# A perceiver layer on one core: weight conversions and lower halves moved from GpSimd to VectorE

## The chip, the core and the metric

The kernel runs on one core of a Trainium2 chip. A core has five engines, each with its own in-order queue of instructions: TensorE (PE in the profile; its weight loads are PEld), VectorE (DVE), ScalarE (ACT), GpSimd (POOL) and SyncE (SP, which here only issues DMA transfers). An instruction starts when those ahead of it on its engine are done and when the semaphores that it waits for, set by other engines or by transfers, have their values.

The metric is the device time of one execution in microseconds (us), lower is better. A run has several executions; the median is given.

## The reference

One perceiver layer: 4 sequences x of 256 tokens and width 256, and a context of 4096 tokens for each. Three blocks, each added to x: cross-attention of x on the context with 16 heads; causal linear attention with positive features; and a gated feed-forward whose weights are stored as int32. The features are the exponential of a clipped projection; the causal attention is the sum over earlier tokens of (qf . kf) v over the same sum without v; `_dequant` multiplies the integers by 1/127. Cut to what matters here:

```python
def _L0_attn_ref(x, Wqkv, bqkv, Wout, bout, omega, quad_nodes, quad_weights):
    ...
    qf = _features(q, omega, quad_nodes, quad_weights)
    kf = _features(k, omega, quad_nodes, quad_weights)
    ...
    return out @ Wout + bout

def _L0_ffn_ref(x, w_gate, w_up, w_down):
    wg = _dequant(w_gate, x.dtype)
    wu = _dequant(w_up, x.dtype)
    wd = _dequant(w_down, x.dtype)
    gate = jnp.einsum('bsd,hd->bsh', x, wg)
    up = jnp.einsum('bsd,hd->bsh', x, wu)
    h = jax.nn.silu(gate) * up
    return jnp.einsum('bsh,dh->bsd', h, wd)

x = x + _L0_xattn_ref(_layernorm(x, axis=-1), ctx_1024, ctx_1024, ...)
x = x + _L0_attn_ref(_layernorm(x, axis=-1), ...)
x = x + _L0_ffn_ref(_layernorm(x, axis=-1), ...)
```

## The kernel before, in words

**Cross-attention.** The 16 head groups (4 sequences x 4 groups of 4 heads; "units") are worked one after the other, each in 16 steps of 256 context tokens. A step n makes the scores `pt` of four heads (L1015 puts the shift in, L1024 the products), ScalarE their exponentials `e` (L1032), and TensorE the weighted values `pav` of the step before (L1046), which VectorE adds to the running sum `av` (L1060). In all units but the last TensorE also makes the maxima for a later unit (`pm`, L955, reduced by VectorE at L961). From about 887 us on, when the maxima are done, the steps of the last unit run, and the work of the later blocks is put between them. These steps are counted here from the first step of the last unit, which is step 0; the ones just before are -1, -2 and so on.

Two dictionaries place this work by step. `plan` holds pieces issued before the step's `pav`, `behind` pieces issued after the step's addition L1060. The order written in the program is the order on TensorE, ScalarE, VectorE and SyncE (it is written out by hand for these four); GpSimd's order follows from it.

**The weights.** The three int32 matrices of the feed-forward (gate, up, down) come in nine pieces of 128x512. `weight_load` (L435-437) has SyncE load piece n into one of two buffers, `wk_sb` for even n and `wv_sb` for odd n. `weight` (L439-441) converts it with GpSimd into `wfr`, in the matmul's type fp32r (integers up to 127 are exact in it). `weight_largest` (L447) has VectorE take the maximum of the converted piece; at the end the maximum of all is read back, and another feed-forward runs if a weight is too large. Piece n is converted in step `made[n]` = -2, -1, 1, 2, 4, 5, 7, 8, 10; right behind it the load of piece n+2 into the same buffer is issued; the maximum follows two steps later. Loads 0 and 1 are issued in step -4.

**Causal attention and feed-forward.** Behind the last unit runs a loop over n = 4 to 16 ("late steps") over the causal attention's head groups, with pieces of the feed-forward and of the output projection filled in (`first` and `fills`). `features` makes four banks `pf` (L314); VectorE clips them (L320), ScalarE takes the exponential (L321), and GpSimd scales the key half (L322). `attend` gives three pieces: the score matmuls `pa` (L340, L345), masked by ScalarE and GpSimd (copy L351, select L352) for two of the four and by VectorE (L357) for the others; the weighted values `po` (L366), copied to `avT` (L372); and, every second group, their transposes `pt_o` (L382) and the division into `att` (L387-389). `output` is two pieces: the transposes `tr_o` of `att` (L406), copied by ScalarE to `oT` (L407), and the projection `py` (L414), added to x by VectorE (L415).

`feed_forward(b)` for sequence b has `norm`, `turn` (transposes `tr_z`, split into an upper half by ScalarE, L621, and a lower half by VectorE, L622), `hidden(m)` for three pieces m and `down(i)` for two row tiles i. To keep fp32 accuracy with fp32r matmuls an activation is split in a half `hi` (rounded to fp32r) and a half `lo` (the rest), and both are multiplied. `hidden(m)`: TensorE makes `pg` and `pu` (L631), ScalarE the tanh (L636), VectorE two products (L637, L638) giving `th`; then GpSimd casts it to `hi` (L646) and subtracts for `lo` (L647), but for the very last piece, where ScalarE casts (L643) and VectorE subtracts (L644). `down(i)` does, for each side, the matmuls of six column blocks (L658), so twelve: first all six with `hi`, then all six with `lo`; blocks 2m and 2m+1 come from piece m. VectorE makes the output row tile (L665), and SyncE sends it (L666).

All matmul results lie in eight PSUM banks that are taken in turn: a new result waits until the one eight before it has been read.

Of the kernel before, what the change touches and what calls it, by code (L numbers as in the profile page):

```python
# [13 lines left out]
F32 = mybir.dt.float32  # L14
F32R = mybir.dt.float32r
I32 = mybir.dt.int32
AF = mybir.ActivationFunctionType
ALU = mybir.AluOpType
# [5 lines left out]
B, T, D = 4, 256, 256  # L24
# [12 lines left out]
NH = HID // P  # L37
# [4 lines left out]
def perceiver_layer(  # L42
# [5 lines left out]
    nc = tc.nc  # L48
# [159 lines left out]
    def bank(shape, name):  # L208

        return psum.tile(shape, F32, tag="b", name=name, bufs=8)  # L210
# [61 lines left out]
    def normed_pieces(tiles):  # L272

        some = nrm[:, tiles[0] : tiles[-1] + 1, :].rearrange("p t h -> p (t h)")
        made = []

        def clipped():
            nc.vector.tensor_scalar(some, some, 1e-24, None, ALU.max)
            y, (first, *others) = inverse_root(some)
            made.extend([*others, lambda: nc.vector.tensor_copy(some, y)])  # L280
            first()

        return [clipped] + 4 * [lambda: made.pop(0)()]
# [145 lines left out]
    def weight_piece(n):  # L429
        if not ws:  # L430
            wfr.append(keep.tile([P, 3 * KC * HID], F32R, tag="wff", name="wfr"))
            ws.extend(parted(wfr[0]))
        return wfr[0][:, n * CH : (n + 1) * CH]
# [4 lines left out]

    def weight(n):  # L439
        to, raw = weight_piece(n), place["raw"][n % 2]  # L440
        nc.gpsimd.tensor_scalar(to, raw.bitcast(I32), 1.0, 1.0, ALU.mult, ALU.mult)


    largest = keep.tile([P, 9], F32, tag="largest", name="largest")
# [34 lines left out]
    behind = {}  # L479

    def start_causal():
# [3 lines left out]
        n = 2 * (B - 1)  # L485
# [39 lines left out]
        def call(f, *args):  # L525
            return lambda: f(*args)
# [37 lines left out]
            15: [step4[1], norm0[3]],  # L564
        }

        made = (-2, -1, 1, 2, 4, 5, 7, 8, 10)
        for n, at in enumerate(made):
            behind.setdefault(at, []).append(call(weight, n))
            if n + 2 < len(made):  # L570
                behind.setdefault(at, []).append(call(weight_load, n + 2))
            behind.setdefault(at + 2, []).append(call(weight_largest, n))
        for b, at in enumerate((-18, -11, -3)):
            for i, piece in enumerate(normed_pieces((2 * b, 2 * b + 1))):
                plan.setdefault(at + i, []).insert(0, piece)
# [22 lines left out]
    def norm_late(z, tiles):  # L598
        for piece in layernorm(z, tiles, True):
            piece()  # L600
        nc.scalar.activation(spare, eps, AF.Tanh)
# [3 lines left out]
    def feed_forward(b):  # L605

        tiles = (2 * b, 2 * b + 1)
        z = work.tile([P, 2, D], F32, tag="z", name="z") if b > 0 else z0
        zT = work.tile([P, 2, KC, T], F32R, tag="zT", name="zT")
        halves_of = []  # L610

        def norm():
            norm_late(lambda t: z[:, t % 2, :], tiles)

        def turn():
            ps = bank([P, KC, 2, P], "tr_z")
            for j in range(2):
                for k in range(KC):
                    nc.tensor.transpose(ps[:, k, j, :], z[:, j, k * P : (k + 1) * P], ident)
            hi, lo = [zT[:, i].rearrange("p k (j t) -> p k j t", t=P) for i in range(2)]  # L620
            nc.scalar.copy(hi, ps)  # L621
            nc.vector.tensor_tensor(lo, ps, hi.bitcast(F32), ALU.subtract)  # L622

        def hidden(m):
            pg, pu = bank([P, 2, T], "pg"), bank([P, 2, T], "pu")
            for side in range(2):
                for ps, w in ((pg, ws[0]), (pu, ws[1])):
                    for i in range(2):
                        ns = slice((2 * m + i) * P, (2 * m + i + 1) * P)
                        for k in range(KC):  # L630
                            nc.tensor.matmul(  # L631
                                ps[:, i, :], lhsT=w[:, k, ns], rhs=zT[:, side, k, :],
                                start=i + k + side == 0, stop=i + k + side == KC + 1,
                            )
            th = work.tile([P, 2, T], F32, tag="th", name="th", bufs=3)
            nc.scalar.activation(th, pg, AF.Tanh, scale=0.5 / 127.0)  # L636
            nc.vector.scalar_tensor_tensor(th, th, 1.0, pg, ALU.add, ALU.mult)  # L637
            nc.vector.tensor_tensor(th, pu, th, ALU.mult)  # L638
            if m == 0:
                halves_of.append(work.tile([P, 2, NH, T], F32R, tag="hT", name="hT", bufs=1))  # L640
            hi, lo = [halves_of[0][:, i, 2 * m : 2 * m + 2, :] for i in range(2)]
            if b == B - 1 and m == NH // 2 - 1:
                nc.scalar.copy(hi, th)  # L643
                nc.vector.tensor_tensor(lo, th, hi.bitcast(F32), ALU.subtract)  # L644
            else:
                nc.gpsimd.tensor_copy(hi, th)  # L646
                nc.gpsimd.tensor_tensor(lo, th, hi.bitcast(F32), ALU.subtract)  # L647

        pds = {}

        def down(i, parts=range(NH)):
            t = tiles[i]
            if i not in pds:
                pds[i] = bank([P, D], "pd")
            pd = pds[i]
            for side in range(2):
                for n in parts:
                    nc.tensor.matmul(  # L658
                        pd, lhsT=halves_of[0][:, side, n, i * P : (i + 1) * P], rhs=ws[2][:, n, :],
                        start=n == 0 and side == 0, stop=n == NH - 1 and side == 1,  # L660
                    )
            if NH - 1 not in parts:
                return
            o = work.tile([P, D], F32, tag="o", name="o")
            nc.vector.scalar_tensor_tensor(o, pd, 0.5 / 127.0**3, xr[:, t, :], ALU.mult, ALU.add)  # L665
            nc.sync.dma_start(out=out[t * P : (t + 1) * P, :], in_=o)  # L666

        return norm, turn, hidden, down


    def feed_forward_any():
# [38 lines left out]
    with tc.manual_schedule(engines={ET.PE, ET.Activation, ET.DVE, ET.SP}):  # L710
        *divide15, project15 = finish
        NB = B * NQ
        norm3, turn3, qk3, sq3, v3, _ = causal_in(3, norm_late)
        ff = {0: feed_forward(0)}
        outputs = [output(b) for b in range(B)]
        ends = normed_pieces((6, 7))
        send, read, compare = weights_large()

        def call(f, *args):
            return lambda: f(*args)  # L720

        def norm(b):
            def begin():
                ff[b] = feed_forward(b)
                ff[b][0]()

            return begin

        def turn(b):
            return lambda: ff[b][1]()  # L730

        def hidden(b, m):
            return lambda: ff[b][2](m)

        def down(b, *args):
            return lambda: ff[b][3](*args)


        first = {
            6: divide15,  # L740
            8: [turn3],
            10: ends[2:] + [call(qk_normed, 6), call(qk_normed, 7)],
            13: [norm(2)],
        }
        fills = {
            4: [turn(0), call(features, 6)],
            5: [hidden(0, 0)],
            6: [call(features, 8), hidden(0, 1), project15, load_root],
            7: [norm3, hidden(0, 2)],
            8: [call(features, 10), call(qk3, 0), down(0, 0), outputs[1][0], call(qk3, 1), outputs[1][1], load_root],  # L750
            9: [norm(1), v3, call(sq3, 0), call(sq3, 1), down(0, 1), *ends[:2], turn(1)],
            10: [hidden(1, 0), call(qk_turned, 6), call(qk_turned, 7), send],
            11: [call(features, 12), hidden(1, 1), read],
            12: [hidden(1, 2), *outputs[2], load_root],
            13: [call(features, 14), down(1, 0), down(1, 1), turn(2)],
            14: [hidden(2, 0), compare],
            15: [hidden(2, 1)],
            16: [
                hidden(2, 2), *outputs[3], load_root, norm(3), down(2, 0), down(2, 1, range(3)), turn(3),
                down(2, 1, range(3, NH)), *[hidden(3, m) for m in range(NH // 2)], down(3, 0), down(3, 1),  # L760
            ],
        }
        steps = [attend(n) for n in range(NB)]
        for n in range(NQ, NB + 1):
            if n > NQ + 1:
                steps[n - 1][1]()
            if NQ < n < NB:
                steps[n][0]()
            for piece in first.get(n, []):
                piece()  # L770
            if n > NQ and n % 2 == 0:
                steps[n - 1][2]()
            for piece in fills[n]:
                piece()
# [676 lines left out]
```

## Time and profile before

| | |
|---|---|
| median of 3 runs | 1066.25 us (1063.87 to 1066.44) |
| the profiled execution's own time | 1064.58 us |
| its span, first to last instruction | 1062.9 us |
| mean granted TensorE clock | 0.992 of full |
| busy, of the span: PE, DVE, ACT, POOL | 97%, 86%, 76%, 20% |
| steps of the last unit with the weights | about 884 to 956 us |
| late steps and the last feed-forward | about 956 to 1058.9 us |
| `weight` L441 on POOL | 9 x 617 ns, 884.4 to 918.1 us |
| cast L646 and subtraction L647 on POOL | 11 x 612 ns and 11 x 1279 ns, 965.0 to 1054.0 us |

The profile is one execution, taken by the hardware's profiler. A timeline row gives start, duration, engine, line, operation, result and operands, their size, the count, and in brackets how long the engine had been idle before it and what ended that. Times count from the span's start. Matmuls overlap, so the ends of TensorE's rows are modelled; the distances of starts are what counts. The granted clock is the share of TensorE's full clock that the chip allowed in a stretch.

### The profile page before, as it was taken

What the parts mean: (1) busy time and instruction counts of PE and PEld (TensorE: products, weight loads), DVE (VectorE), ACT (ScalarE), POOL (GpSimd) and SP (SyncE); (2) the same over time, 40 slices, a digit from 0 to 9 for tenths busy, and PEclk for the clock granted to TensorE, in tenths of its full rate; (3) what the DMA queues carried; (4) which work ended last, traced back from release to release, by engine and by line L of the source; (5) the groups of instructions that cost most, each with busy time, mean ns of one, the idle gap of its engine ahead of it and who ended that gap; (6) DMA issues with size and microseconds to landing.
All of it is one profiled execution on the core that took longest, in us unless ns stands there. A gap on an engine that the chain in (4) does not pass through costs nothing.

```text
span 1062.9 us, 45087 instructions
## 1 busy us (share of the span) xinstructions
PE 1028.1 (97%) x19032; PEld 716.1 (67%) x19032; DVE 917.1 (86%) x1771; ACT 808.7 (76%) x1678; POOL 215.8 (20%) x308
## 2 busy tenths in 40 slices
PE   6999999999999999999999999999999998998997
PEld 3457667766776677667766776677666666566676
DVE  3998999999899999999999999999998996577775
ACT  3348888888888888888888888878885677785463
POOL 3422220032003200320032003201232102205343
PEclk8999999999999999999999999999999999999999
DMA  8666574366435753574357536643473301200000
GB/s 250 178 161 173 111 191 127 98 134 169 122 103 116 180 129 102 108 192 127 101 114 190 125 97 134 173 110 100 109 174 91 71 14 34 61 3 12 11 12 22
DMA packets 93791, 120.31 MB, mean 113 GB/s; under 512 B 49561, under 2 KB 58642, under 8 KB 93586
## 3 DMA queue, kind: packets, MB, share of 16 engines
q1 hardware_dynamic: 92738, 116.59, 44.0%
q8 instruction: 152, 2.49, 1.0%
q10 hardware_dynamic: 720, 0.79, 0.2%
q14 instruction: 53, 0.43, 0.2%
q0 software_dynamic: 128, 0.00, 0.0%
HBM read 76.25 MB, written 3.33 MB: 75 GB/s over the span
## 4 chain that ended last, share of the span: by engine, by line
PE 84%; DVE 9%; DMA 2%; ACT 1%; issue 1%; SPq 1%; POOL 1%; ACTq 0%; DVEq 0%; POOLq 0%
PE pc L184 23%; PE pav L1046 20%; PE pm L955 17%; PE pt L1024 11%; DVE mx L961 5%; PE pt L1015 4%; PE pqk L184 1%; PE pa L340 1%; PE po L366 1%; PE py L414 1%; PE pg L631 1%; PE pu L631 1%; PE py L184 1%; ACT feat L321 1%; PE pa L345 0%
## 5 line engine op out<-in xcount | busy, mean ns | idle before, releaser
L961 DVE TENSOR_REDUCE mx<-pm 128x1 f32<-128x512 f32 x787 | 506.1, 684 | 47.6 <-PE pm L955 44.1
L1032 ACT ACTIVATE e<-pt 128x512 f32<-128x512 f32 x1024 | 530.7, 614 | 15.7 <-PE pt L1024 15.2
L955 PE MATMUL pm<-kt,qa 32*128 32x512 f32 x2048 | 355.8, 426 | 9.2 <-DMA kt<-khl 5.7
L1024 PE MATMUL pt<-qa,kt 32*128 32x256 f32 x4096 | 283.3, 278 | 0.0
L1024 PEld LDWEIGHTS pt<-qa,kt 32*128 32x128 f32 x4096 | 270.4, 184 | 7.2
L1046 PE MATMUL pav<-e,v 128*32 128x256 f32 x4096 | 270.8, 381 | 0.7 <-issue 0.7
L955 PEld LDWEIGHTS pm<-kt,qa 32*128 32x128 f32 x2048 | 163.0, 191 | 120.6 <-ACT e L1032 82.3
L1015 PE MATMUL pt<-sh,ones 2*128 2x512 f32 x1024 | 226.0, 449 | 0.8 <-ACT e L1032 0.4
L1046 PEld LDWEIGHTS pav<-e,v 128*32 128x32 f32 x4096 | 129.2, 110 | 73.3 <-issue 4.7
L857 POOL CAST khl<-ku 128x512 fp32r<-128x512 f32 x63 | 38.5, 611 | 516.3 <-ACT ku L877 483.1
L184 PE MATMUL pc<-wff,wk_sb 128*32 128x256 f32 x2048 | 138.2, 392 | 0.0
L184 PE MATMUL pc<-wv_sb,wff 128*32 128x128 f32 x4096 | 137.6, 276 | 0.1
L965 ACT COPY copy<-pm 128x512 f32<-128x512 f32 x119 | 69.8, 587 | 65.8 <-PE pm L955 65.8
L965 ACT COPY wff<-pm 128x512 f32<-128x512 f32 x118 | 69.3, 587 | 65.9 <-PE pm L955 65.9
L184 PEld LDWEIGHTS pc<-wv_sb,wff 128*32 128x32 f32 x4096 | 104.4, 109 | 20.9 <-ACT copy L965 8.5
L1060 DVE TENSOR_TENSOR av<-pav,av 128x256 f32<-128x256 f32 x240 | 101.3, 422 | 15.9 <-PE pav L1046 6.4
L1015 PEld LDWEIGHTS pt<-sh,ones 2*128 2x128 f32 x1024 | 93.3, 182 | 13.1 <-ACT e L1032 3.5
L184 PEld LDWEIGHTS pc<-wff,wk_sb 128*32 128x32 f32 x2048 | 55.4, 111 | 46.6 <-ACT copy L965 8.7
L858 POOL TENSOR_TENSOR khl<-ku,khl 128x512 fp32r<-128x512 f32 x63 | 80.7, 1281 | 5.0
L961 DVE TENSOR_REDUCE mx<-copy 128x1 f32<-128x512 f32 x119 | 80.4, 675 | 0.0
L961 DVE TENSOR_REDUCE mx<-wff 128x1 f32<-128x512 f32 x118 | 79.6, 675 | 0.0
L877 ACT ACTIVATE ku<-pc,bk_sb 128x256 f32<-128x256 f32 x128 | 64.8, 508 | 14.9 <-PE pc L184 11.1
(160 smaller groups left out, 731.8 us busy)
## 6 DMA issues: line engine op xcount, KB each, us to landing
wff<-in_ctxT_dram SPq DMA_DIRECT2D x128, 512.0 KB
kt<-khl SPq DMA_DIRECT2D x254, 128.0 KB
qa<-qhl SPq DMA_DIRECT2D x64, 64.0 KB
scr<-av SPq DMA_DIRECT2D x16, 128.0 KB
oT<-scr SPq DMA_DIRECT2D x128, 8.0 KB
xr<-in_x_dram SPq DMA_DIRECT2D x4, 256.0 KB
dn<-sums SPq DMA_DIRECT2D x32, 32.0 KB
out_dram<-o SPq DMA_DIRECT2D x8, 128.0 KB
```

The source lines that it names most:

```text
L184: nc.tensor.matmul(out[js], lhsT=lhsT[:, js], rhs=rhs, **flags)
L857: engine.tensor_copy(hi, x)
L858: engine.tensor_tensor(lo, x, hi.bitcast(F32), ALU.subtract)
L877: nc.scalar.activation(ku[:, cs], made.pop(), AF.Identity, bias=bk_sb[:, m : m + 1])
L955: nc.tensor.matmul(pm, lhsT=qa[rows, turn, i::2], rhs=kt[rows, :], start=turn == 0, stop=turn == 1)
L961: nc.vector.tensor_reduce(mx[:, i, j, c : c + 1], of[j], AX.X, ALU.max)
L965: nc.scalar.copy(to, pms[heads.index(j)])
L1015: nc.tensor.matmul(pt, lhsT=ones[rows, :], rhs=sh[rows, :].unsqueeze(1).to_broadcast([2, 2, T]), start=True, stop=False,)
L1024: nc.tensor.matmul(pt[:, i, :], lhsT=kt[rows, k0 : k0 + P], rhs=qa[rows, turn], start=False, stop=i == 1 and turn == 1,)
L1032: nc.scalar.activation(e, pt, AF.Exp, scale=0.25)
L1046: nc.tensor.matmul(pav[32 * h : 32 * h + 32, :], lhsT=v[:, t % KT, c0 : c0 + 32], rhs=es[n, h][:, i, :], start=i == 0, stop=i == 1,)
L1060: nc.vector.tensor_tensor(avs[u], pav, avs[u], ALU.add)
```

## The change

```diff
@@ weight @@
         to, raw = weight_piece(n), place["raw"][n % 2]
-        nc.gpsimd.tensor_scalar(to, raw.bitcast(I32), 1.0, 1.0, ALU.mult, ALU.mult)
+        nc.vector.tensor_copy(to, raw.bitcast(I32))
@@ start_causal @@
-        made = (-2, -1, 1, 2, 4, 5, 7, 8, 10)
-        for n, at in enumerate(made):
-            behind.setdefault(at, []).append(call(weight, n))
-            if n + 2 < len(made):
-                behind.setdefault(at, []).append(call(weight_load, n + 2))
-            behind.setdefault(at + 2, []).append(call(weight_largest, n))
+        for n, (sent, made) in enumerate(((-4, -2), (-4, -1), (-1, 2), (-1, 3), (3, 6), (3, 7), (7, 9), (7, 10), (10, 12))):
+            if n > 1:
+                behind.setdefault(sent, []).append(call(weight_load, n))
+            behind.setdefault(made, []).append(call(weight, n))
+            behind.setdefault(made + 1, []).append(call(weight_largest, n))
@@ feed_forward @@
-        halves_of = []
+        halves_of, ths = [], {}
...
             nc.vector.tensor_tensor(th, pu, th, ALU.mult)
             if m == 0:
                 halves_of.append(work.tile([P, 2, NH, T], F32R, tag="hT", name="hT", bufs=1))
+            ths[m] = th
+            hi = halves_of[0][:, 0, 2 * m : 2 * m + 2, :]
+            (nc.scalar.copy if b == B - 1 and m == NH // 2 - 1 else nc.gpsimd.tensor_copy)(hi, th)
+
+        def lower(m):
             hi, lo = [halves_of[0][:, i, 2 * m : 2 * m + 2, :] for i in range(2)]
-            if b == B - 1 and m == NH // 2 - 1:
-                nc.scalar.copy(hi, th)
-                nc.vector.tensor_tensor(lo, th, hi.bitcast(F32), ALU.subtract)
-            else:
-                nc.gpsimd.tensor_copy(hi, th)
-                nc.gpsimd.tensor_tensor(lo, th, hi.bitcast(F32), ALU.subtract)
+            nc.vector.tensor_tensor(lo, ths.pop(m), hi.bitcast(F32), ALU.subtract)
@@ the late steps @@
-            6: [call(features, 8), hidden(0, 1), project15, load_root],
-            7: [norm3, hidden(0, 2)],
-            8: [call(features, 10), call(qk3, 0), down(0, 0), outputs[1][0], call(qk3, 1), outputs[1][1], load_root],
+            6: [call(features, 8), hidden(0, 1), lower(0, 0), project15, load_root],
+            7: [norm3, hidden(0, 2), lower(0, 1)],
+            8: [
+                call(features, 10), call(qk3, 0), lower(0, 2), outputs[1][0], call(qk3, 1), down(0, 0),
+                outputs[1][1], load_root,
+            ],
             9: [norm(1), v3, call(sq3, 0), call(sq3, 1), down(0, 1), *ends[:2], turn(1)],
             10: [hidden(1, 0), call(qk_turned, 6), call(qk_turned, 7), send],
-            11: [call(features, 12), hidden(1, 1), read],
-            12: [hidden(1, 2), *outputs[2], load_root],
-            13: [call(features, 14), down(1, 0), down(1, 1), turn(2)],
+            11: [call(features, 12), hidden(1, 1), lower(1, 0), read],
+            12: [hidden(1, 2), lower(1, 1), *outputs[2], load_root],
+            13: [call(features, 14), lower(1, 2), down(1, 0), down(1, 1), turn(2)],
             14: [hidden(2, 0), compare],
-            15: [hidden(2, 1)],
+            15: [hidden(2, 1), lower(2, 0)],
             16: [
-                hidden(2, 2), *outputs[3], load_root, norm(3), down(2, 0), down(2, 1, range(3)), turn(3),
-                down(2, 1, range(3, NH)), *[hidden(3, m) for m in range(NH // 2)], down(3, 0), down(3, 1),
+                outputs[3][0], hidden(2, 2), lower(2, 1), outputs[3][1], load_root, norm(3), lower(2, 2), down(2, 0),
+                down(2, 1, range(3)), turn(3), down(2, 1, range(3, NH)), hidden(3, 0), hidden(3, 1), lower(3, 0),
+                hidden(3, 2), lower(3, 1), lower(3, 2), down(3, 0), down(3, 1),
             ],
```

- The conversions go from GpSimd (multiplication by 1 twice) to VectorE (a copy). Piece n is sent in one step and converted in a later one, two to four steps apart: loads 2 and 3 are issued in step -1, 4 and 5 in step 3, 6 and 7 in step 7, 8 in step 10. The maximum follows one step behind the conversion.
- `hi` is still cast by GpSimd (the last piece by ScalarE). `lo` is a piece of its own, `lower(b, m)`, on VectorE, placed by hand behind the next piece or later.
- Three orders are changed: `down(0, 0)` goes behind the second `qk3` in step 8; the transposes `outputs[3][0]` go ahead of `hidden(2, 2)` in step 16; and in step 8 `outputs[1][0]` goes ahead of `down(0, 0)`.
- In the loop of the late steps `first[13]`, which is `norm(2)`, is issued ahead of `fills[13]`, and `norm(3)` stands in step 16 ahead of `lower(2, 2)`.

More of the change, by code (lines that the diff above doesn't have):

```diff
@@ L666, in down @@
             nc.sync.dma_start(out=out[t * P : (t + 1) * P, :], in_=o)
-        return norm, turn, hidden, down
+        return norm, turn, hidden, down, lower
     def feed_forward_any():
@@ L733, in hidden, with lower @@
             return lambda: ff[b][2](m)
+        def lower(b, m):
+            return lambda: ff[b][4](m)
         def down(b, *args):
```

## The prediction

> **What bounds the kernel now.** I read the page first, then TensorE's waits, then the timeline at each wait, then the clock there.
>
> ```profile
> PE 1028.1 (97%) x19032; PEld 716.1 (67%) x19032; DVE 917.1 (86%) x1771; ACT 808.7 (76%) x1678; POOL 215.8 (20%) x308
> ...
> PE 84%; DVE 9%; DMA 2%; ACT 1%; issue 1%; SPq 1%; POOL 1%; ACTq 0%; DVEq 0%; POOLq 0%
> ```
>
> The page's busy times and its chain that ended last: TensorE (PE) works 97% of the span and 84% of the chain is its own. So a stall of TensorE is paid in full; idle time elsewhere is free. The change touches only what comes after about 884 us of 1062.9. There TensorE's waits are (line, releaser, total, times, longest, in us):
>
> ```profile
> PE po L366 <- POOL at L352: 4.2, 3, 2.1
> PE pa L340 <- POOL feat L322: 2.7, 2, 2.5
> PE tr_qk L292 <- DVE qk L287: 2.2, 1, 2.2
> ```
>
> The first two come from GpSimd (POOL). In the timeline (start, duration, engine, instruction, idle before it) the weight conversion L441 stands ahead of each long one:
>
> ```profile
> 896.56 0.62 POOL L441 TENSOR_SCALAR wfr<-wk_sb 128x512 fp32r<-128x512 int32 x1 [5.06 <-DMA wk_sb<-in_w_gate_dram]
> ...
> 897.69 0.70 PE L340 MATMUL pa<-feat 64*128 64x256 f32 x4 [2.47 <-POOL feat L322]
> ...
> 918.11 0.62 POOL L441 TENSOR_SCALAR wfr<-wk_sb 128x512 fp32r<-128x512 int32 x1 [2.16 <-DMA wk_sb<-in_w_down_dram]
> ...
> 919.14 1.86 PE L366 MATMUL po<-at,va 128*32 128x256 f32 x16 [2.15 <-POOL at L352]
> ```
>
> GpSimd sat waiting for a weight to land, and L322 and L352, which TensorE needed, were queued behind it. The stall is not the whole price. By stretches (busy us of each engine, then the granted clock):
>
> ```profile
> 898.00:901.00 3.00, 3.00 (x28) 1.49 (x28) 1.42 (x4) 0.00 (x0) 1.86 (x5) 0.57 0.00 0
> 919.00:922.00 3.00, 2.86 (x22) 1.77 (x24) 0.00 (x0) 0.52 (x2) 0.44 (x2) 0.50 0.02 5
> 1003.30:1006.00 2.70, 2.70 (x24) 1.40 (x24) 2.53 (x7) 1.17 (x2) 0.00 (x0) 0.68 0.00 0
> ```
>
> After each stall of 2.15 to 2.47 us the clock is 0.50 to 0.68 for some 3 us, then 0.72 to 0.95 for 3 more. 3 x 0.43 + 3 x 0.14, 3 x 0.50 + 3 x 0.05 and 2.7 x 0.32 + 3 x 0.28 are 1.7, 1.65 and 1.7 us. After shorter stalls (1.39 us at 963, 1.0 at 974) it stays at 1.00.
>
> **The weights.** Nine GpSimd conversions (0.617 us each) and their waits go, so L322 and L352 follow ScalarE at once.
> First stall: ScalarE is then the limit. It has eight exponentials until 896.68 and two `at` copies until 897.44; the fourth score bank of step 0 is the first copy's, so step 0 starts at about 897.0, not 900.46. It also runs at full clock; following its banks the same way, step 1 starts at 901.5, not 905.28: **-3.8** (bounds: the stall alone, -2.5; stall and clock, -4.2).
> Second: `po` of step 4 can start when its scores end, 917.0, not 919.14, and step 5 at 920.3, not 924.17: **-3.9** (-2.15 to -4.0).
>
> VectorE gets nine copies of 128x512, int32 to fp32r, within SBUF. No row has this. The nearest are VectorE's cast of the same shape from f32, 427 ns, and its copy from PSUM (L295), 685 ns. I take 0.43, so 3.9 us in all (6.2 at most). VectorE is busy 3.6 of 9 us at 897-906, 8.3 of 12 at 906-918, 4.5 of 12 at 918-930, so there they cost nothing. At 930-943 and 943-956 it is busy 10.2 and 10.1 of 13: there the running sum L1060 of step 12 comes 0.4 to 0.7 us later (one conversion and one maximum L448 more ahead of it), and the fourth `pa` bank of step 13 waits for it. **+0.2** (0 to 0.5). Without that idle time, up to 6.2.
> Their loads still wait for the conversion two before, but land 2.6 to 2.9 us after issue (rows of `wk_sb`) and are used two or more steps (4 us and more) later: no wait; with one, everything behind on VectorE (L1060, feature clips) would stand for up to 2.9. On SP the loads of the second and third matrix go behind the `dn` reads and all but the first two behind the `oT` reads, and `oT` now waits for the conversion of step 3; `oT` is not used until 942.92, some 28 us later: nothing.
>
> **The lower halves.** Twelve subtractions, 1.279 us on GpSimd (L647), become 0.692 us on VectorE; the row (busy, mean ns) is that of the one that was VectorE's already:
>
> ```profile
> L644 DVE TENSOR_TENSOR hT<-th,hT 128x512 fp32r<-128x512 f32 x1 | 0.7, 692 | 0.7 <-ACT hT L643 0.7
> ```
>
> VectorE takes its queue in order, so what counts is what stands ahead of and behind each.
>
> Late steps 6 to 8: GpSimd's L352 before `po` (977.03) starts 1.27 earlier, but VectorE's lower half (0,0) now precedes L1114, L357 and the normalisation, so ScalarE's root, table load and tanh (978.66) come 0.69 later, and with them L637 and L638 (ended 980.75), which free the banks of `pt_o` and `pf`: `pf` at 981.5, not 980.77. (0,1) and (0,2) fit: (0,2) ends at about 988.05, and down-projection (0,0), now behind both `pqk`, reaches the matmul that needs it, its eleventh, then. **+0.75** (-0.6, the earlier `po` alone, to +1.4, both lower halves).
>
> Step 12: (1,0) stands between L638 (ends 1015.2) and L357, whose chain to `att` and `tr_o` is the one that ended last: **+0.7** (0 to 0.7).
>
> Step 13: here is the largest term. Lower half (1,2) is issued after the four clips of the next features; the down-projection needs it from its eleventh matmul on.
>
> ```profile
> 1023.10 3.09 PE L658 MATMUL pd<-wfr,hT 128*128 128x256 f32 x24
> ...
> 1025.45 2.96 DVE L320 TENSOR_SCALAR feat<-pf,low,top 128x512 f32<-128x512 f32 x4
> ...
> 1028.33 0.74 DVE L665 SCALAR_TENSOR_TENSOR o<-pd,xr 128x256 f32<-128x256 f32 x2
> ```
>
> L665, whose matmuls were done by 1026, had to wait for the clips until 1028.33; the lower half takes that place and ends at 1029.02. TensorE does ten matmuls (3.09/24 = 0.129 each) to 1024.4, then stalls 4.6 us. From 1029.07: 14 matmuls 1.8, `tr_z` 0.6, `po` 0.79, `pa` 1.55, `pt_o` 0.58 give the next hidden layer at 1034.4, against 1030.40 in the chain (which had waits of its own): 4.0, and 1.65 of clock: **+5.65** (4.0 to 6.3).
>
> Step 16: `tr_o` moves ahead of the hidden layer (2,2), and (2,0) stands before `att`. TensorE is free at 1038.72 and `att` ends at 1040.02: 1.3 us of stall that the hidden layer used to cover. The output projection starts at 1042.58 instead of 1041.33. VectorE then has (2,1) ahead of the residual, so z ends at 1048.26, not 1046.17, and (2,2) behind z ends at 1048.9. The down-projection (2,0) stops after ten matmuls, at 1045.9, for 3.0 us; behind it eight matmuls (1.03), `tr_z` (0.6) and six (0.77) end at 1051.35, against 1047.38: 4.0, and 1.65 of clock: **+5.6** (2.7, without the move of `tr_o`, to 6.2).
>
> Tail: (3,0) stands before L637 of (3,2): **+0.2** (0 to 0.7); GpSimd's casts are earlier but not last.
>
> **The sum.** -3.8 - 3.9 + 0.2 + 0.75 + 0.7 + 5.65 + 5.6 + 0.2 = +5.4 us. On the profiled execution (1064.58, span 1062.9) that is 1070.0; on the median of the runs (1066.25, the higher side of 1063.87 to 1066.44) 1071.65. I take 1071. All low ends give -2.1, all high ends +11.1; about two thirds of the way out, the sum lies between +1 and +9: 1065 to 1075.
>
> The Trainium skill, "TensorE: Matmul & The Clock Gate", "HAM oscillation — how this bites in real kernels", has the clock drop only after idle gaps above about 3.4 us. The rows above show drops after 2.15 to 2.47, so they decide; by the page the removed stalls would bring 4.65 instead of 7.7, step 16 would cost 1.65 less, and the sum would be +6.8. "SBUF — State Buffer", "Who interferes with whom", speaks against the change: a VectorE instruction with two SBUF inputs blocks a GpSimd one that reads SBUF, and the lower half is such. In the trace two L322 beside L287 at 911 take 1.36 us together instead of 0.96. By the rule one L352 ahead of `po` could lose up to 0.69 more: +6.1.
>
> **Rivals.**
> (a) Faster: the lower halves stay hidden. If (1,2) and (2,2) reached TensorE within the 1.3 us of the first ten matmuls, steps 13 and 16 would cost only the 1.25 of `tr_o`: +5.4 - 5.65 - 5.6 + 1.25 = -4.6, 1061. For it: VectorE has 0.5 us idle at 1023-1029. Against: z and the clips stand ahead in the same queue and wait for `pa` and `pf`. It decides below 1.3 us of lateness; I count 4.6 and 3.0. Chance 0.11.
> (b) No change: one of the two stalls is as counted, the other mostly covered because everything behind it was late anyway (1026 to 1030 already had waits on `feat` and `avT`): +5.4 - 4.5 = +1, 1066.5. Chance 0.21.
> (c) Conversions block: VectorE waits for a weight, or is full at 930-956, and takes the place of GpSimd's wait: one load's 2.9 more, +8.3, 1074. Against: idle time and margins above. Chance 0.10.
> (d) GpSimd's wait isn't gone, since L322 and L352 still wait for ScalarE: if only the stalls proper shrink by half, the first two terms are -1.25 and -1.1, +10.7, 1076. Chance 0.05.
> My forecast has 0.53. A difference under 0.3%, 3.2 us, can't be told from none here. Slower: the forecast, (c) and (d), 0.68; within: 0.21; faster: 0.11.
>
> **What would show it.** No POOL L441, and no stall at 897 or 919, with the clock at 1.00 from 897 to 925. Down-projection split after ten matmuls twice, waiting for VectorE's subtraction 4.6 and 3.0 us, with a clock near 0.5 behind each; `tr_o` waiting 1.3 us for `att`. If the two `pd` groups run unbroken, or the clock stays up behind them, I am wrong by 4 to 11 us.

## The result, and the profile after

| | before | after |
|---|---|---|
| median of 9 runs each, on one chip | 1066.25 us (1063.07 to 1067.39) | 1068.75 us (1066.23 to 1070.91) |
| ratio of after to before, with its 95% interval | | 1.0032 [1.0018, 1.0046] |
| the profiled execution's own time, its span | 1064.58, 1062.9 us | 1070.05, 1068.2 us |
| first `pf` of the last unit (step -3) to `po` of step 15: "early" | 65.15 us | 57.67 us |
| from there to the last group of `pd`: "late" | 102.65 us | 114.24 us |

The kernel became slower by 0.32%, 3.4 us of 1066.25 (1.9 to 4.9). This ratio weighs all runs; the two medians alone are 2.5 us apart. The last two rows of the table, read from TensorE's timeline (starts of the groups named), tell why: the stretch with the weights is 7.5 us shorter, the stretch with the lower halves 11.6 us longer, 4.1 us in sum. The rows that they are read from, first before, then after:

```profile
888.00 1.12 PE L314 MATMUL pf<-qkT,om_sb 32*128 32x256 f32 x16
953.15 0.86 PE L366 MATMUL po<-at,va 128*32 128x256 f32 x16
1055.80 2.66 PE L658 MATMUL pd<-wfr,hT 128*128 128x256 f32 x20 [1.31 <-ACT hT L643]
...
889.36 1.13 PE L314 MATMUL pf<-qkT,om_sb 32*128 32x256 f32 x16
947.03 0.86 PE L366 MATMUL po<-at,va 128*32 128x256 f32 x16
1061.27 2.65 PE L657 MATMUL pd<-wfr,hT 128*128 128x256 f32 x20 [1.07 <-ACT hT L642]
```

The two traces also differ by 1.36 us ahead of the first of these rows. Two traces of one and the same kernel (runs 1 and 1b below) differ there by 1.13, so this is not put down to the change; distances of starts leave it out.

In the changed kernel the lines behind the weights are shifted: the cast to `hi` is L642, the lower half L646, the down-projection `pd` L657, its output L664. The busy times and the chain that ended last, after:

```profile
PE 1028.7 (96%) x19032; PEld 717.4 (67%) x19032; DVE 927.3 (87%) x1791; ACT 808.8 (76%) x1678; POOL 200.6 (19%) x288
...
PE 85%; DVE 11%; ACT 2%; issue 1%; DMA 1%; ACTq 0%; POOL 0%; SPq 0%; DVEq 0%; POOLq 0%
```

TensorE's work is the same. In the chain GpSimd and SyncE's queue each go from 1% to 0% and the transfers from 2% to 1%, while VectorE has 11% instead of 9%: one limit was exchanged for another. TensorE's waits from 878 us on (line, releaser, total, times, longest):

```profile
PE pd L657 <- DVE hT L646: 6.7, 2, 4.5
PE tr_o L406 <- DVE att L389: 2.5, 2, 1.3
PE tr_qk L292 <- DVE qk L287: 2.2, 1, 2.2
PE po L366 <- POOL at L352: 1.4, 1, 1.4
```

The two waits on L322 and L352 at 897 and 919 us are gone (the 1.4 left is one at 957 that was there before). In their place TensorE waits 6.7 us for lower halves, in two pieces. The timeline shows both:

```profile
1017.96 1.44 PE L657 MATMUL pd<-wfr,hT 128*128 128x256 f32 x10
...
1020.30 2.96 DVE L320 TENSOR_SCALAR feat<-pf,low,top 128x512 f32<-128x512 f32 x4
1023.18 0.68 DVE L646 TENSOR_TENSOR hT<-th,hT 128x512 fp32r<-128x512 f32 x1
...
1023.92 3.35 PE L657 MATMUL pd<-wfr,hT 128*128 128x256 f32 x14 [4.51 <-DVE hT L646]
...
1045.97 0.98 PE L657 MATMUL pd<-wfr,hT 128*128 128x256 f32 x6 [0.60 <-POOL hT L642]
...
1048.40 0.68 DVE L646 TENSOR_TENSOR hT<-th,hT 128x512 fp32r<-128x512 f32 x1
...
1049.14 2.08 PE L657 MATMUL pd<-wfr,hT 128*128 128x256 f32 x8 [2.19 <-DVE hT L646]
```

Step 13: the down-projection stops after ten matmuls, VectorE does four clips and only then the lower half. The 14 matmuls behind the stall take 3.35 us, against 3.09 for all 24 before. Step 16: four matmuls and six (ten again), and 2.19 us of wait. The stretches of the profile (start and end, length, busy us of PE, PEld, DVE, ACT, POOL with counts, then the granted clock) show how the clock went, in the stretch of the weights, behind `tr_qk`, and around step 13:

```profile
897.00:906.00 9.00, 9.00 (x147) 5.70 (x147) 6.58 (x16) 7.23 (x17) 1.57 (x4) 1.00 0.23 70
906.00:918.00 12.00, 12.00 (x182) 7.92 (x182) 7.90 (x18) 10.27 (x22) 4.01 (x8) 1.00 0.21 54
918.00:930.00 12.00, 12.00 (x211) 8.10 (x204) 8.10 (x18) 9.58 (x21) 0.02 (x1) 1.00 0.19 49
...
997.00:1000.00 3.00, 2.28 (x16) 1.74 (x20) 2.83 (x7) 1.01 (x2) 0.00 (x0) 0.64 0.00 0
...
1021.00:1024.00 3.00, 0.08 (x1) 0.08 (x1) 2.86 (x5) 2.85 (x4) 1.56 (x3) 0.63 0.00 0
1024.00:1027.00 3.00, 3.00 (x14) 3.00 (x15) 0.42 (x1) 0.02 (x1) 0.66 (x2) 0.50 0.13 44
1027.00:1030.00 3.00, 3.00 (x32) 2.10 (x32) 1.12 (x2) 0.96 (x2) 0.00 (x0) 0.74 0.13 44
```

From 897 to 930 TensorE is busy throughout, at full clock. Around 1024 the clock is down from within the stall until 1029.

### The profile page after: what moved, and what is told of

Its sections match the earlier page's. It is cut to its first block, busy times and chain, and to the rows that moved or that the text cites. A ratio compares the mean times of both kernels' runs of the same rounds, so it can differ in the third digit from the quotient of the medians.

```text
span 1068.2 us, 45085 instructions
## 1 busy us (share of the span) xinstructions
PE 1028.7 (96%) x19032; PEld 717.4 (67%) x19032; DVE 927.3 (87%) x1791; ACT 808.8 (76%) x1678; POOL 200.6 (19%) x288
## 4 chain that ended last, share of the span: by engine, by line
PE 85%; DVE 11%; ACT 2%; issue 1%; DMA 1%; ACTq 0%; POOL 0%; SPq 0%; DVEq 0%; POOLq 0%
PE pc L184 23%; PE pav L1052 20%; PE pm L961 17%; PE pt L1030 11%; DVE mx L967 5%; PE pt L1021 4%; PE pqk L184 1%; PE pa L340 1%; PE pd L657 1%; PE po L366 1%; ACT feat L321 1%; PE py L184 1%; DVE at L357 1%; PE py L414 1%; PE tr_qk L292 0%
## 5 line engine op out<-in xcount | busy, mean ns | idle before, releaser
L1066 DVE TENSOR_TENSOR av<-pav,av 128x256 f32<-128x256 f32 x240 | 101.5, 423 | 15.6 <-PE pav L1052 6.1
```

The lines of the kernel that those rows point to most:

```text
L1066: nc.vector.tensor_tensor(avs[u], pav, avs[u], ALU.add)
```

## The experiments

The theory is the prediction's: the weights' part wins 7.5 us by itself, the lower halves lose more, and they lose it by their place in VectorE's queue. The rivals: the terms are not independent (what is won early is given back by waits that were there anyway), or VectorE lacks the time for the lower halves wherever they stand. Ratios are to the kernel before, run in the same series on the same chip; "early" and "late" are the two distances of the table above, from each run's own trace. In some traces the clock also drops behind the wait of `tr_qk` at about 1000 us, in others not (the last section); that is 1.7 us of "late", so it has a column.

| run | median, us | ratio, 95% interval | early | late | drop at `tr_qk` |
|---|---|---|---|---|---|
| before | 1066.25 | | 65.15 | 102.65 | yes |
| after | 1068.75 | 1.0032 [1.0018, 1.0046] | 57.67 | 114.24 | yes |
| 1 weights alone | 1056.37 | 0.9928 [0.9903, 0.9952] | 57.66 | 101.05 | no |
| 1b the same again | 1054.83 | 0.9887 [0.9869, 0.9905] | 57.65 | 102.49 | yes |
| 2 lower halves alone | 1075.54 | 1.0107 [1.0079, 1.0134] | 64.37 | 114.60 | yes |
| 3 lower(1,2) sooner | 1062.59 | 0.9981 [0.9965, 0.9997] | 57.67 | 108.56 | yes |
| 4 step 16 reordered | 1064.47 | 1.0000 [0.9984, 1.0015] | 57.68 | 109.16 | no |
| 5 both | 1058.48 | 0.9948 [0.9931, 0.9965] | 57.65 | 103.00 | no |
| 6 VectorE, old steps | 1056.74 | 0.9939 [0.9921, 0.9956] | 57.42 | 102.31 | yes |
| 7 GpSimd, new steps | 1068.94 | 1.0052 [1.0034, 1.0070] | 71.89 | 101.07 | no |
| 8 stalls filled | 1065.43 | 1.0015 [1.0004, 1.0027] | 57.66 | 109.29 | no |
| 9 all places mended | 1057.09 | 0.9909 [0.9893, 0.9925] | 57.65 | 101.47 | no |
| 10 mixed | 1056.10 | 0.9907 [0.9886, 0.9928] | 57.68 | 100.80 | no |

Runs 1 to 4 are one series and 5 to 8 a second, both on the chip numbered 13; 1b, 9 and 10 are a third, on chip 4. The medians of before in these series were 1064.29, 1063.89 and 1066.12 us.

### 1 and 1b. The weights alone

```diff
 # the kernel before, with the change's weight() and its table of (sent, made)
-        nc.gpsimd.tensor_scalar(to, raw.bitcast(I32), 1.0, 1.0, ALU.mult, ALU.mult)
+        nc.vector.tensor_copy(to, raw.bitcast(I32))
```

> Only the weights' part of the change (conversion on VectorE, the new load and conversion steps); the lower halves on GpSimd and all orders as before. Theory: the two early terms of the sum and the conversions stand alone, -3.9 - 4.0 + 0.4 = -7.5 us against the kernel before, ratio 0.993; no wait at L340 or L366 behind GpSimd at 897 and 919, clock 1.00 at 897 to 925. Rival 1: what was saved early is given back by waits that the late steps had anyway (feat and avT at 1026 to 1030): -3 to -4, ratio 0.997. Rival 2: the pause only moves, as VectorE now stands for the weights: 0 or worse, ratio 1.000 or above.

> The weights' part alone once more, the same kernel as in the first series, for a comparison on one chip: ratio 0.991 to 0.994. If it stands clearly under the kernel with all lower halves mended, VectorE's lower halves cost something wherever they are put; if level, only their places did.

"Early" falls by 7.5 us in both traces, and "late" stays as it was (102.49 against 102.65, both with the drop behind `tr_qk`; 101.05 without). Nothing is given back. The two ratios, 0.9928 and 0.9887, are of one kernel, in two series on two chips, and 0.4% apart, with intervals that just touch; smaller differences between series are not read here.

### 2. The lower halves alone

```diff
 # the changed kernel, with the weights and their steps as before
-        nc.vector.tensor_copy(to, raw.bitcast(I32))
+        nc.gpsimd.tensor_scalar(to, raw.bitcast(I32), 1.0, 1.0, ALU.mult, ALU.mult)
```

> Only the other part (lower halves on VectorE, the three changed orders); weights on GpSimd as before. Theory: the terms of steps 6 to 8, 12, 13, 16 and the tail add up as in the changed kernel's trace, 0.55 + 0.6 + 6.0 + 4.8 - 0.2 = +11.7 us against the kernel before, ratio 1.011; the down-projection is split after ten matmuls in steps 13 and 16. Rival: the late terms exist only because the late steps start earlier in the changed kernel, when ScalarE and VectorE are not yet ready: then +4 to +6, ratio 1.004 to 1.006.

1.0107, where 1.011 was expected; "late" grows by 11.95 us, as in the changed kernel (11.59). The split down-projections are there unchanged, though the late steps start later:

```profile
1022.51 1.44 PE L658 MATMUL pd<-wfr,hT 128*128 128x256 f32 x10
1028.46 3.35 PE L658 MATMUL pd<-wfr,hT 128*128 128x256 f32 x14 [4.51 <-DVE hT L647]
```

Same ten matmuls, same 4.51 us. So the two parts add up: -0.72% and +1.07% make +0.35%, against 0.32% measured. The traces say the same: -7.5 us of "early" and +11.95 of "late" make +4.5, against 4.1 in the changed kernel. ("Early" is 0.8 us shorter here than in the kernel before, though the weights are as they were: its trace has one drop of the clock there instead of two.)

### 3. lower(1,2) sooner

```diff
-            12: [hidden(1, 2), lower(1, 1), *outputs[2], load_root],
-            13: [call(features, 14), lower(1, 2), down(1, 0), down(1, 1), turn(2)],
+            12: [hidden(1, 2), lower(1, 1), *outputs[2], lower(1, 2), load_root],
+            13: [call(features, 14), down(1, 0), down(1, 1), turn(2)],
```

> The changed kernel, with lower(1,2) moved from behind the four clips of step 13 to the end of step 12, behind the output projection's additions and ahead of the scores' L357, where VectorE is idle for 1.9 us. Theory: place in VectorE's queue alone makes the stall; the 24 matmuls of the down-projection run unbroken and the step-13 term goes, -6.0 us against the changed kernel, so -2.5 to -3.5 against the kernel before, ratio 0.997. Rival: the stall is covered elsewhere, since tr_z or the next scores then wait for the clips and for L664 behind them: -1 to -3, ratio 1.000 to 1.002.

TensorE's row in that trace is whole again:

```profile
1015.45 3.09 PE L657 MATMUL pd<-wfr,hT 128*128 128x256 f32 x24
```

From `py` of step 12 to `po` of late step 15 it is 14.44 us before, 20.41 after and 14.44 here: moving one instruction of 0.68 us up in VectorE's queue takes back all of the 5.97. No other wait takes its place there. The ratio, 0.9981, lies between the theory's 0.997 and the rival's 1.000, so it is the trace that decides.

### 4. Step 16 reordered

```diff
-                outputs[3][0], hidden(2, 2), lower(2, 1), outputs[3][1], load_root, norm(3), lower(2, 2), down(2, 0),
+                hidden(2, 2), lower(2, 1), outputs[3][0], lower(2, 2), outputs[3][1], load_root, norm(3), down(2, 0),
```

> The changed kernel with step 16 put in another order: tr_o back behind hidden(2,2), and lower(2,2) ahead of the residual addition and norm(3). Theory: -4.8 us against the changed kernel (1.3 of tr_o, 2 of the split down-projection, the rest clock), so -1.5 to -2 against the kernel before, ratio 0.998 to 0.999. Rival: lower(2,2) ahead of z makes z 0.7 us late and the transposes behind it too, so that only -2 to -3 is won: ratio 1.000 to 1.001.

The ratio, 1.0000, is the rival's, though its interval reaches to the theory's; the trace lies between the two. From `po` of late step 16 to the first `pg` of the last sequence it is 10.69 us before, 15.38 after and 11.40 here: 4.0 of 4.7 come back. The timeline shows what keeps the rest:

```profile
1041.24 2.49 PE L657 MATMUL pd<-wfr,hT 128*128 128x256 f32 x18
...
1044.69 0.73 DVE L127 TENSOR_SCALAR z<-xr,ln_mv,ln_rs 128x256 f32<-128x256 f32 x2
...
1045.25 0.67 PE L618 MATMUL tr_z<-ident,z 128*128 128x128 f32 x4 [1.52 <-DVE z L127]
```

The 18 matmuls run unbroken, but both lower halves now stand ahead of z, and `tr_z` waits 1.52 us for it (0.29 before): here the rival's mechanism is real, at 0.7 us.

### 5. Both places

The edits of 3 and 4 together.

> The changed kernel with both mended places: lower(1,2) at the end of step 12, and step 16 in the order of the earlier run (tr_o behind hidden(2,2), lower(2,2) ahead of the residual addition). Theory: the terms are independent, so 6.0 + 4.0 us come off the changed kernel (1.0032 of before) and what is left is the weights' gain less 0.55 (steps 6 to 8), 0.6 (step 12) and 0.7 (z late in step 16): -5.5 to -6.5, ratio 0.994 to 0.995. Rival: the down-projections and their neighbours find the next limit on VectorE, which now does all twelve lower halves, and part of the stalls comes back in step 14 to 16: -3 to -4, ratio 0.996 to 0.997.

0.9948, as the sum of independent terms asked. "Late" is 2.0 us longer than in run 1, both without the drop at `tr_qk`, where 0.55, 0.6 and 0.7 (1.85 in all) were left to come: no part of the stalls comes back elsewhere.

### 6. One line: VectorE, at the old steps

```diff
 # the kernel before, nothing else changed
-        nc.gpsimd.tensor_scalar(to, raw.bitcast(I32), 1.0, 1.0, ALU.mult, ALU.mult)
+        nc.vector.tensor_copy(to, raw.bitcast(I32))
```

> The kernel before with one line changed: weights converted by VectorE, at the steps they had. Theory: what stalls TensorE before is that GpSimd reaches a conversion early and stands there for the load; VectorE reaches it only behind that step's addition, at about 905 for the load that lands at 896.5, so the engine alone removes both stalls: -6.5 to -7.5 us, ratio 0.993 to 0.994. Rival (VectorE waits for the loads, which the new steps were needed to avoid): a wait of 2 to 5 us on VectorE in which TensorE stands for its additions, so 0 to +3, ratio 1.000 to 1.003.

"Early" is 57.42 us: the engine alone takes both stalls away. The timeline (load issued, then its conversion) shows why:

```profile
893.44 0.38 SPq L437 DMA_DIRECT2D wk_sb<-in_w_gate_dram  x1
...
906.48 0.41 DVE L441 CAST wfr<-wk_sb 128x512 fp32r<-128x512 int32 x1
```

VectorE reaches this conversion 13 us behind the load's issue, without a wait, since its own queue is full until then. GpSimd, with little else to do, had been there 5 us too soon.

### 7. GpSimd, at the new steps

```diff
 # the kernel before, with the change's table of (sent, made) only
-        made = (-2, -1, 1, 2, 4, 5, 7, 8, 10)
+        for n, (sent, made) in enumerate(((-4, -2), (-4, -1), (-1, 2), (-1, 3), (3, 6), (3, 7), (7, 9), (7, 10), (10, 12))):
```

> The kernel before with only the steps of loads and conversions changed; the conversions stay on GpSimd. Theory: the loads are sent two to four steps ahead, so GpSimd finds them landed and only its own 0.62 us per conversion stands before L322 or L352: -5 to -7 us, ratio 0.9935 to 0.9955. Rival: GpSimd, with little to do, still runs ahead to the conversion and waits for the load with L322 or L352 behind it: 0 to -3, ratio 0.997 to 1.000.

Both missed: 1.0052, and "early" is 6.7 us longer than before. The rival had the mechanism but not its size:

```profile
912.68 4.94 SPq L1090 DMA_DIRECT2D oT<-scr  x8
...
917.72 0.40 SPq L437 DMA_DIRECT2D wk_sb<-in_w_down_dram  x1
...
920.48 0.62 POOL L441 TENSOR_SCALAR wfr<-wk_sb 128x512 fp32r<-128x512 int32 x1 [3.75 <-DMA wk_sb<-in_w_down_dram]
...
923.88 0.62 POOL L441 TENSOR_SCALAR wfr<-wk_sb 128x512 fp32r<-128x512 int32 x1 [2.14 <-DMA wk_sb<-in_w_down_dram]
924.45 0.77 POOL L352 TENSOR_SCALAR_AFFINE_SELECT at<-at 128x256 f32<-128x256 f32 x2
...
924.92 1.86 PE L366 MATMUL po<-at,va 128*32 128x256 f32 x16 [6.55 <-POOL at L352]
```

GpSimd still runs ahead of the other engines to its conversions. The later loads now stand in SP's queue behind eight reads of `oT` (912.7 to 917.6; before, they were issued between these reads, at 910.7 to 915.4), so GpSimd waits for them longer, with L352 queued behind. The new steps do not mend the stall; on GpSimd they make it worse.

### 8. The stalls filled with useless matmuls

```diff
             pd = pds[i]
+            for _ in range({1: 34, 2: 21}.get(b, 0) if i == 0 else 0):
+                nc.tensor.matmul(pd, lhsT=halves_of[0][:, 0, 0, :P], rhs=ws[2][:, 0, :], start=True, stop=True)
```

> The changed kernel with useless matmuls ahead of two down-projections: 34 of the pd kind (128x128 by 128x256, 0.129 us each) ahead of down(1,0), 21 ahead of down(2,0), into the same bank and overwritten. They fill the stalls of 4.5 and 2.2 us, so TensorE waits no less for the lower halves but does not pause. Theory: the clock's drop behind a pause is a price of its own, 1.65 us for the first and about 1.2 for the second: -2 to -3 us against the changed kernel though it does 7 us more work, ratio 1.000 to 1.001; granted clock 1.00 at 1024 to 1030. Rival: the clock drops for another reason (the load on the chip, not the pause): no gain or a loss, ratio 1.003 to 1.005.

The timeline and the stretches around step 13:

```profile
1015.87 4.26 PE L656 MATMUL pd<-wfr,hT 128*128 128x256 f32 x34
1019.96 1.34 PE L659 MATMUL pd<-wfr,hT 128*128 128x256 f32 x10
1021.82 1.91 PE L659 MATMUL pd<-wfr,hT 128*128 128x256 f32 x14 [0.52 <-DVE hT L646]
```

```profile
1016.00:1019.00 3.00, 3.00 (x26) 3.00 (x27) 2.53 (x9) 1.78 (x3) 0.00 (x0) 1.00 0.00 0
1019.00:1022.00 3.00, 2.48 (x21) 2.27 (x20) 2.77 (x5) 2.88 (x4) 1.66 (x3) 1.00 0.00 0
1022.00:1025.00 3.00, 3.00 (x36) 2.46 (x38) 1.03 (x3) 0.59 (x1) 0.57 (x2) 1.00 0.13 44
```

The last 14 matmuls start 7.03 us behind `pf`, as in the changed kernel, but take 1.91 us instead of 3.35, and the clock stays at 1.00. `py` to `po` of late step 15 is 18.32 us instead of 20.41, and the stretch in step 16 is 13.98 instead of 15.38: what the clock cost behind the pauses is 2.09 and 1.40 us. From 880 us to the last matmul this trace has no drop at all. More work, less time. By the ratios the gain is 0.17% (about 1.8 us, as uncertain as it is large, and less than the 3.5 of the trace); 1.0015 lies between the theory's 1.001 and the rival's 1.003. So the trace carries this, and the ratios agree only in sign.

### 9. All lower halves on VectorE, each in an idle place

```diff
-            6: [call(features, 8), hidden(0, 1), lower(0, 0), project15, load_root],
-            7: [norm3, hidden(0, 2), lower(0, 1)],
+            6: [call(features, 8), hidden(0, 1), project15, load_root],
+            7: [norm3, lower(0, 0), hidden(0, 2), lower(0, 1)],
...
+            12: [lower(1, 0), hidden(1, 2), lower(1, 1), *outputs[2], lower(1, 2), load_root],
...
+                lower(2, 1), hidden(2, 2), outputs[3][0], outputs[3][1], lower(2, 2), load_root, norm(3), down(2, 0),
```

> The changed kernel with all twelve lower halves still on VectorE, each put where VectorE is idle: (0,0) behind the normalisation of step 7, (1,0) behind att in step 12, (1,2) at the end of step 12, (2,1) ahead of hidden(2,2), (2,2) behind the residual additions, tr_o behind hidden(2,2). Theory: the terms of steps 6 to 8 and 12 go as well (-0.5 and -0.6 against the run with two places mended) and z in step 16 comes 0.5 sooner: ratio 0.993 to 0.994, level with the weights' part alone. Also, where a lower half no longer stands beside it, GpSimd's cast L642 takes 0.61 us instead of 1.00: pieces (0,1), (1,1) and (2,2). Rival: ratio stays at 0.995 because VectorE's own work, 12 x 0.6 us more, sets the end; and the cast stays at 1.00.

The lower halves' cost goes away place by place: `po` of step 15 to `po` of late step 9 is 36.39 us before, 36.94 after, 36.38 here; `pf` to `py` around step 12 is 9.49, 10.09, 9.49; step 16 is 10.69, 15.38, 11.01. The ratio is below what was expected, as is that of 1b on the same chip, 0.9887; 9 against 1b is +0.22%, which the intervals don't separate from nothing. GpSimd's casts:

```profile
1006.07 0.61 POOL L642 CAST hT<-th 128x512 fp32r<-128x512 f32 x1 [0.46 <-DVE th L637]
1007.68 0.68 DVE L646 TENSOR_TENSOR hT<-th,hT 128x512 fp32r<-128x512 f32 x1
...
1009.67 0.68 DVE L646 TENSOR_TENSOR hT<-th,hT 128x512 fp32r<-128x512 f32 x1
1009.82 1.00 POOL L642 CAST hT<-th 128x512 fp32r<-128x512 f32 x1 [2.78 <-DVE th L637]
```

The cast of (1,1) stands alone and takes 0.61 us; that of (1,2) begins 0.15 us behind a lower half and takes 1.00. In the changed kernel (1,1) took 1.00 too; (0,1) and (2,2) went from 1.00 to 0.61 in the same way.

### 10. Mixed: (2,1) and (2,2) back on GpSimd

```diff
-            nc.vector.tensor_tensor(lo, ths.pop(m), hi.bitcast(F32), ALU.subtract)
+            engine = nc.gpsimd if b == 2 and m > 0 else nc.vector
+            engine.tensor_tensor(lo, ths.pop(m), hi.bitcast(F32), ALU.subtract)
```

Besides, (2,1) is issued in step 15, right behind its hidden layer, and (2,2) in step 16 right behind its own; the rest is as in run 9.

> As the run with all places mended, but the lower halves (2,1) and (2,2) back on GpSimd, as before the change, since VectorE has z to make there. Theory: tr_z of step 16 no longer waits for z (1.5 us there with two places mended, 1.0 with all mended): 0.7 to 1.0 us less than that run, ratio 0.992 to 0.993. Rival: GpSimd's 1.28 us for each holds the down-projection (2,0) instead, no gain: ratio 0.994.

`tr_z` waits 0.4 us instead of 1.0, and step 16 takes 10.40 us instead of 11.01: 0.6 us, where 0.7 to 1.0 was expected. The medians can't tell it from run 9. The versions that beat both kernels are 1, 3, 5, 6, 9 and 10, run 3 only just. Among the other five the ratios show no difference beyond that between series; the traces, all set without the drop at `tr_qk`, have run 5 last, at 103.0 us of "late" against 100.6 to 101.5. Run 6 is one line.

## Why the prediction was right, and where it was off

It said slower, 1071 us (1065 to 1075), and the median is 1068.75. The mechanism was the one forecast, with -7.5 early and about +12 late; in the traces the sum is +4.1 instead of +5.4, and over all runs the ratio gives +3.4 (1.9 to 4.9), little more than the 3.2 us that the prediction called the least that can be told from none. That the profiled execution took 1070.05 us, where 1070.0 was forecast, is luck: 1.36 us of it lie ahead of all the terms. Its steps, as numbers of the prediction against distances in the traces:

| step | forecast, us | measured, us | shown by |
|---|---|---|---|
| first stall, L322 behind the conversion | -3.8 | -4.0 | 1, 6 |
| second stall, L352 behind the conversion | -3.9 | -3.9 | 1, 6 |
| conversions on VectorE | +0.2 | +0.4 | 1; in 6, at the old steps, 0.0 |
| late steps 6 to 8 | +0.75 | +0.55 | 9 takes it back |
| step 12, (1,0) ahead of `att` | +0.7 | +0.60 | 9 takes it back |
| step 13, (1,2) behind the clips | +5.65 | +5.97 | 3 takes it back |
| step 16 | +5.6 | +4.69 | 4 takes 4.0 back |
| tail | +0.2 | -0.05 | trace of after |

- **The weights.** Right in place and size. But the prediction put it down to the new steps (loads that are "used two or more steps (4 us and more) later") that no conversion on VectorE would wait for its load. In run 6 none of the nine waits at the old steps either, so the engine does it alone; run 7 shows that the new steps alone cost 6.7 us of "early". The copies took 0.417 us (eight of nine), near the 0.43 assumed.
- **Steps 6 to 8.** The size was right, the path was not: `pf` of step 8 was forecast 0.73 late and came on time (27.55 us behind `po` of step 15 before, 27.59 after), since the earlier `po` (by 0.78 us) made up for it; the 0.55 shows only at `po` of late step 9.
- **Step 13.** The stall was 4.51 us (4.6 forecast), and what was paid for the clock 2.09 (1.65 forecast). The lost clock is 3.42 us in that trace, but part of it falls into the stall, where it costs nothing.
- **Step 16: the term that was mis-sized.** The prediction had the down-projection stop 3.0 us for (2,2) and 1.65 us of clock. TensorE stopped 0.60 us earlier in that group, for GpSimd's cast, then 2.19 us for (2,2), and paid 1.40 for the clock (run 8). That the clock fell behind a pause as short as 2.19 us was not certain (the last section), though it did in all three traces that have this pause. The wait of `tr_o` was 1.33, as forecast 1.3.
- **Rivals.** (a), lower halves hidden, falls with 4.51 and 2.19 us of wait. (b), one of the two stalls mostly covered, falls with runs 3 and 4, where each gives 6.0 and 4.0 back. (c) falls since no conversion waited for its load and "early" is shorter by all that was forecast. (d) falls with a stretch at full clock and no wait from 897 to 930.

## What to carry to other kernels

An instruction that waits for a transfer is best put on an engine whose queue is long enough that it comes late by itself (run 6); on an idle engine with an in-order queue it arrives too soon and holds what stands behind it, and planning the loads elsewhere can make that worse (run 7). Moving work to a faster engine pays by its place in that engine's queue, not by its duration: 0.68 us put behind four clips cost 6.0, and put into an idle gap nothing (run 3); all twelve in idle places (run 9) cost 0.4 us of "late" against run 1, and nothing that the medians could tell. When a part of a change gains and another loses, split it before keeping or dropping it.

## What the runs showed of the hardware

**The clock falls by whole steps, and not after every pause.** With the clock read in steps of 0.5 us in all thirteen traces from 880 us on, no lone pause of TensorE up to 1.53 us was followed by a drop; of nineteen pauses of 2.15 to 2.47 us eleven were and eight were not, each of the eleven with the same loss, 1.70 to 1.71 us of full-speed time (3.4 us at 0.50); pauses of 2.87, 3.05, 4.51 (three times) and 6.55 us lost 3.42, 1.70, 3.42 and 5.12. Once, in run 5, the clock fell at 1051 us behind short pauses close together (0.70 and 1.07 us among them), which made its last group of matmuls 3.67 us long instead of 2.65; seven other traces have the same two pauses and no drop. The wait of `tr_qk` is 2.18 or 2.19 us in all thirteen traces and has the drop in six; of runs 1 and 1b, the same kernel, one has it and the other not.

So the length of a pause alone doesn't decide. The traces show what does: where the pause lies on a fixed grid. In each trace all drops of the clock, 54 in the thirteen, start whole multiples of 3.413 us apart (in after at 997.86, 1021.75 and 1049.06, so 7 and then 8 times 3.413). Cut into stretches on that grid, the time around the wait of `tr_qk` looks as follows, first in after, then in run 9:

```profile
994.45:997.86 3.41, 1.22 (x10) 1.04 (x11) 3.17 (x11) 0.60 (x1) 0.00 (x0) 1.00 0.00 0
997.86:1001.27 3.41, 3.41 (x26) 2.23 (x27) 2.43 (x7) 1.40 (x3) 0.61 (x1) 0.50 0.01 2
...
991.27:994.68 3.41, 1.98 (x15) 1.58 (x13) 3.17 (x12) 0.60 (x1) 0.00 (x0) 1.00 0.00 0
994.68:998.09 3.41, 2.43 (x28) 1.71 (x30) 3.20 (x8) 1.51 (x3) 0.00 (x0) 1.00 0.00 0
998.09:1001.50 3.41, 3.41 (x43) 2.87 (x40) 2.55 (x6) 1.26 (x4) 1.40 (x3) 1.00 0.05 7
```

In after the whole pause lies in one stretch, TensorE is busy for 1.22 us of it, and the next stretch runs at 0.50. In run 9 the pause is split between two stretches, with 1.98 and 2.43 us of work, and the clock stays. It is so with all nineteen: ahead of the eleven drops TensorE was busy for 0.94 to 1.49 us of the stretch, and in the other eight cases for no less than 1.71 us of any stretch that the pause touches. The bound isn't sharp by this count, since the drop in run 5 followed 1.77 us of work and one in run 7 (at 896 us) 2.00. Where the grid lies differs between executions, so it makes a term of the sum uncertain by 1.7 us that no reading of the trace of before can settle.

The Trainium skill, "TensorE: Matmul & The Clock Gate", "HAM oscillation — how this bites in real kernels", has the clock fall for idle gaps above about 3.4 us; eleven drops here followed gaps of 2.15 to 2.47, so as a bound for safety it is too high. Part 1 of the same page, "The HAM clock gate (the "warmup" mystery)", speaks of a free-running window of 3413 ns, which agrees with losses of 1.71 us and its multiples, and with the 3.413 us between the starts of the drops.

**A lower half on VectorE slows a cast on GpSimd beside it.** Seven of the eleven casts of the changed kernel took 1.00 us, all that began 0.15 us behind a lower half; the four others took 0.61, and run 9 turned three of the seven into 0.61 by moving the lower halves. The rule weighed in the prediction (the Trainium skill, "SBUF — State Buffer", "Who interferes with whom") thus holds here, at 0.39 us for a 128x512 cast; what it cost TensorE was smaller: the last `pd` group but one waited 0.70 us for the cast instead of 0.39. The 0.60 us of step 16 was for such a cast too, but the longer wait for the lower half came right behind it.
